# Keeping GpSimd's one-hots and token scatters in traced order, with one scatter in three turns

## The chip, the cores and the metric

The kernel runs on one core of a Trainium2 chip. A core has five engines that each work through their own queue in order: TensorE (PE, matrix products), VectorE (DVE), ScalarE (ACT), GpSimd (POOL) and SyncE (SP, which here only starts transfers). Engines wait for each other by semaphores. The metric is device time in microseconds (us) of one execution, as the median of several runs; less is better. Profiled times are counted from the start of the span of one profiled execution.

## The reference, cut to what matters

Four layers follow each other, each added to x (6250 nodes, 256 features, 100,000 edges). The change is in the seam between the first two.

```python
x = x + gcn(layernorm(x), edges, edge_weight)       # weighted sum over edges, by source; then a two-layer MLP
x = x + moe8(layernorm(x)[None])[0]                 # router, two best of 8 experts
x = x + rgcn(edges, layernorm(x), edge_type)        # sum over edges, by destination
x = x + moe6(layernorm(x)[None])[0]                 # router, two best of 6 experts
```

The sum of the first layer and the router of the second:

```python
msgs = xw[col_sl] * norm[:, None]
h7 = jax.ops.segment_sum(msgs, row_sl, num_segments=N) + b
h = jax.nn.relu(h7 @ W1 + b1)
out = h @ W2 + b2
...
logits = tokens.astype(jnp.float32) @ router_w.astype(jnp.float32).T
probs = jax.nn.softmax(logits, axis=-1)
rw, re = jax.lax.top_k(probs, TOP_K)
```

## The kernel before

Nodes are cut into 49 blocks of 128. An earlier stage has written the message of every edge to device memory (`msgs`), sorted by the block of its source, in 830 tiles of 128 messages. The stage that the change touches, called "sums by source" here, sums them and at the same time starts on the second layer.

`sum_messages` (L944 to L988) takes one tile of messages per **turn**. For a turn, a 128 x 128 one-hot matrix says which row of the block each message belongs to; PE multiplies it with the messages (L983, two passes in the profile), and DVE adds the product to the block's columns of `acc` (L985). Turns go in batches of eight. For each batch one load brings the messages (L950, SP's queue, three batches ahead) and `one_hots` (L953 to L971) makes eight one-hots `m`: DVE computes the keys (L956, marked to keep its order) and makes the first two (L958), ACT the next two (L967 and L968), POOL the last four, one instruction each (L970). The one-hots of the next batch are traced after the second turn of the running one; `m` has two buffers. After every turn the generator yields.

`sum_and_send` (L1270 to L1294) calls `step` once per turn. When a group of four blocks is complete (due at turn 16.46 times the blocks done so far, plus 12, so about every 66 turns), `send_group` starts for it, and each step runs it on to its next `yield`. For four blocks `send_group` works through these steps:

- scale the sums, transpose, MLP, add to X, mean and variance (L1161 to L1191): 11 yields
- normalised tokens `tok` on ACT (L1199), transposes, router products `pl` (L1208): 6 yields
- `route` (L1038 to L1076, with `top`, L1020): a chain of small operations, on DVE but for one exponential on ACT (L1054): 2 yields
- ranks of the tokens at their experts: `both`, `seen` (L1222 to L1231), two small matmuls into `prk` (L1237 and L1240), `place` (L1245 to L1249), and the places in two integer tables `at1` and `at2`, both parts of `ats` (L1255): 2 yields
- the scatters: for each of the four blocks, two indirect transfers issued by POOL (L1259) write its 128 tokens to their two places in `xs`. Before, one yield stands ahead of each pair, so that a group sends two scatters per turn in four turns.

That is 25 yields for a group of four. There are 13 groups: twelve of four blocks and one of one. The last two finish after the last turn. The second layer's experts start when all scatters have landed.

What sets the order: the program is traced in Python, and the framework's scheduler then fixes each engine's queue from the traced order and the dependences, and may put an instruction ahead of or behind others that it doesn't depend on. `tc.keep_in_program_order` marks an instruction that is to keep its traced order among the marked ones of its engine. Before, in this stage, only the keys (L956) are marked. Transfers issued by POOL share its queue with the one-hots. The scatters depend on `tok`, `ats` and nothing else in the stage.

Of the kernel before, what the change touches and what calls it, by code (L numbers as in the profile page):

```python
# [15 lines left out]
OP = mybir.AluOpType  # L16
# [41 lines left out]
def gnn_ffn_kernel(ctx: ExitStack, tc: tile.TileContext, a, out):  # L58
    nc = tc.nc
# [7 lines left out]
    def psum_mm(name):  # L67
        return p_mm.tile([128, 512], F32, tag="mm", name=name)
# [63 lines left out]
    minus = const.tile([128, 128], F32, name="minus")  # L132
# [43 lines left out]
    def blocks_of(blk, t0, engines, top):  # L176
        _, v = nc.values_load_multi_w_load_instructions(
            blk[0:1, t0 : t0 + 8],
            engines=engines,
            min_val=0,  # L180
            max_val=top,
            skip_runtime_bounds_check_because="it is counted or bounded",
        )
        return v
# [176 lines left out]
    with tc.If(unsorted > 0):  # L361
        with tc.tile_pool(name="reorder", bufs=1) as rp:
# [40 lines left out]
            for c in range(EC):  # L403
                ins = nc.gpsimd.indirect_dma_start(
                    out=records,
                    out_offset=bass.IndirectOffsetOnAxis(ap=pos_i[:, c : c + 1], axis=0),
                    in_=rec[:, c, :],
                    in_offset=None,
                )
# [534 lines left out]
    def sum_messages(pool, tag):  # L944

        def take(t0):
            g = pool.tile([128, 8, RW], F32, name=f"g0{tag}_{t0}", tag="g", bufs=4)
            nc.sync.dma_start(g, by_tile[:, t0 : t0 + 8, :])  # L950
            return g

        def one_hots(t0, g):  # L953
            n = min(8, T - t0)
            key = pool.tile([128, 8], F32, name=f"key{tag}{t0}", tag="key")
            tc.keep_in_program_order(nc.vector.tensor_sub(key[:, :n], firsts[:, t0 : t0 + n], g[:, :n, D]))  # L956
            m = pool.tile([128, 8, 128], F32, name=f"m0{tag}_{t0}", tag="m", bufs=2)
            nc.vector.tensor_tensor(  # L958
                m[:, :2],
                minus[:, None, :].to_broadcast([128, 2, 128]),  # L960
                key[:, :2, None].to_broadcast([128, 2, 128]),
                OP.is_equal,
            )
            for j in range(2, n):
                if j < 4:
                    far = pool.tile([128, 128], F32, name=f"far{tag}{t0}_{j}", tag="far", bufs=2)
                    nc.scalar.activation(far, lanes, AF.Abs, bias=key[:, j : j + 1])  # L967
                    nc.scalar.activation(m[:, j], far, AF.Relu, bias=ones[:, 0:1], scale=-1.0)  # L968
                else:
                    nc.gpsimd.tensor_scalar(m[:, j], minus, key[:, j : j + 1], None, op0=OP.is_equal)  # L970
            return m  # L971

        come = {t0: take(t0) for t0 in (0, 8, 16)}
        ready = one_hots(0, come[0])
        for t0 in range(0, TL, 8):
            n = min(8, T - t0)
            blocks = blocks_of(blks, t0, [ENG.DVE], NT)
            if t0 + 24 < TL:
                come[t0 + 24] = take(t0 + 24)
            g, m = come.pop(t0), ready  # L980
            for j in range(n):
                ps = psum_mm(f"pa0{tag}_{t0 + j}")
                nc.tensor.matmul(ps[:, :D], m[:, j, :], g[:, j, :D], start=True, stop=True)  # L983
                here = acc[:, bass.ds(blocks[j] * D, D)]
                nc.vector.tensor_add(here, here, ps[:, :D])  # L985
                if j == 1 and t0 + 8 < TL:
                    ready = one_hots(t0 + 8, come[t0 + 8])
                yield t0 + j + 1  # L988
# [163 lines left out]
    def send_group(g, n, mlp, tag, seen):  # L1152
# [97 lines left out]
        for k, (at, oh) in enumerate(((at1, oh1), (at2, oh2))):  # L1250
            p1 = mlp.tile([128, n], F32, name=f"p{tag}{g}_{k}", tag="p1", bufs=2)
            nc.vector.tensor_reduce(p1, oh, axis=AX.X, op=OP.add)
            if g + n == NT:
                nc.vector.tensor_add(p1[:, n - 1 :], p1[:, n - 1 :], nobody)
            nc.vector.tensor_copy(at[:, g : g + n], p1)  # L1255
        for i, t in enumerate(tiles):
            yield
            for at in (at1, at2):
                ins = nc.gpsimd.indirect_dma_start(  # L1259
                    out=xs,  # L1260
                    out_offset=bass.IndirectOffsetOnAxis(ap=at[:, t : t + 1], axis=0),
                    in_=tok[:, i, :],
                    in_offset=None,
                    bounds_check=8 * CAP - 1,
                    oob_is_err=False,
                )
                tc.declare_no_dep(ins.ins, group=f"tokens{tag}", reason="every token has a place of its own")
                tc.add_to_no_dep_group(f"tokens{tag}", ins.ins)

    def sum_and_send(tag, early):  # L1270


        with (
            tc.tile_pool(name=f"sum{tag}", bufs=3, side="right") as sump,
            tc.tile_pool(name=f"mlp{tag}", bufs=1) as mlp,
        ):
            seen, steps, waiting = [], None, list(GROUPS)

            def step(through):
                nonlocal steps  # L1280
                if steps is None and waiting and through(sum(waiting[0])):
                    g, n = waiting.pop(0)
                    steps = send_group(g, n, mlp, tag, seen)
                if steps is not None and next(steps, steps) is steps:
                    steps = None

            for turn in sum_messages(sump, tag):
                if turn % 8 == 0 and 5 <= turn // 8 < 13:
                    e = turn // 8 - 5
                    nc.sync.dma_start(fw1[:, e], a["L0_ffn_w1"][e].rearrange("(k p) f -> p k f", p=128))  # L1290
                if early:
                    step(lambda blocks: S_TURNS * blocks + S_SLACK <= turn)
            while steps is not None or waiting:
                step(lambda blocks: True)  # L1294
# [66 lines left out]
    for e in range(8):  # L1361
        eng = nc.scalar if e % 2 else nc.sync
        ins = eng.dma_start(xs[bass.ds(ends[e], 128), :], zeros)
# [382 lines left out]
```

## Time and profile before

| | us |
|---|---|
| median of 15 runs | 4037.45 (4034.43 to 4045.95) |
| profiled execution, its time | 4038.73 |
| profiled execution, its span | 4036.9 |

By stretches of that span (busy us of each engine in it):

| stretch, us | what runs | PE | DVE | ACT | POOL | PE clock |
|---|---|---|---|---|---|---|
| 0 to 330 | sorting by source, x times W | 262 | 241 | 146 | 41 | 0.91 |
| 330 to 1280 | most of the messages | 742 | 152 | 348 | 728 | 0.93 |
| 1335 to 2005 | sums by source, with the dispatch | 551 | 494 | 207 | 339 | 0.93 |
| 2030 to 2330 | experts of the second layer | 264 | 111 | 116 | 40 | 0.95 |
| 2700 to 4037 | sums by destination, last experts | 1241 | 759 | 292 | 849 | 0.95 |

How to read it: the busy time is the time in which an engine had an instruction running; the PE clock is the share of its full clock that was granted. Lines of the profile name the engine, the source line, the operation, the tile it writes and the tiles it reads; in brackets stands the idle time ahead of it and what ended that. In the timeline, instructions of one line that follow each other without a pause are merged ("x4").

### The profile page before, as it was taken

What the parts mean: (1) busy time and instruction counts of PE and PEld (TensorE: products, weight loads), DVE (VectorE), ACT (ScalarE), POOL (GpSimd) and SP (SyncE); (2) the same over time, 40 slices, a digit from 0 to 9 for tenths busy, and PEclk for the clock granted to TensorE, in tenths of its full rate; (3) what the DMA queues carried; (4) which work ended last, traced back from release to release, by engine and by line L of the source; (5) the groups of instructions that cost most, each with busy time, mean ns of one, the idle gap of its engine ahead of it and who ended that gap; (6) DMA issues with size and microseconds to landing.
All of it is one profiled execution on the core that took longest, in us unless ns stands there. A gap on an engine that the chain in (4) does not pass through costs nothing.

```text
span 4036.9 us, 53283 instructions
## 1 busy us (share of the span) xinstructions
PE 3430.6 (85%) x14649; PEld 2290.6 (57%) x14649; DVE 2036.7 (50%) x5609; ACT 1322.3 (33%) x3006; POOL 2256.0 (56%) x2450
## 2 busy tenths in 40 slices
PE   7968877777787678888789779996789999999999
PEld 5756656565566355555567534442456666666656
DVE  6872111111111567777723387664556666666552
ACT  3714333333333133233234335662112222221213
POOL 1007777777777455555420185335767777777740
PEclk9989999989999899999899889997889999999999
DMA  3435333333333555555443354446555555555530
GB/s 119 169 106 169 128 126 128 127 128 129 127 129 125 214 180 194 189 193 191 160 127 109 98 188 196 188 203 218 150 140 152 154 147 157 150 151 150 148 108 9
DMA packets 227434, 602.88 MB, mean 149 GB/s; under 512 B 40620, under 2 KB 121689, under 8 KB 207276
## 3 DMA queue, kind: packets, MB, share of 16 engines
q0 software_dynamic: 100736, 295.11, 23.5%
q1 hardware_dynamic: 108242, 287.41, 20.7%
q10 hardware_dynamic: 18138, 16.68, 1.2%
q8 instruction: 132, 2.16, 0.2%
q14 instruction: 186, 1.52, 0.1%
HBM read 362.97 MB, written 236.11 MB: 148 GB/s over the span
## 4 chain that ended last, share of the span: by engine, by line
PE 47%; DVE 14%; DMA 11%; issue 7%; POOL 4%; ACT 3%; DVEq 1%; POOLq 0%; ACTq 0%; SPq 0%
DMA msgs<-msgn,at 8%; PE ph_e1a L246 6%; PE pa1a L1012 6%; PE py1a L1091 6%; PE ph_e2a L246 5%; PE pxn L908 5%; PE phx L1509 4%; PE pa0e L983 4%; DVE acc L985 4%; PE pf L1428 2%; PE pf L1444 2%; POOL msgs L926 2%; DVE rest L1519 1%; DVE sTn L891 1%; DVE acc L1016 1%
## 5 line engine op out<-in xcount | busy, mean ns | idle before, releaser
L1004 POOL DMA_INDIRECT g1a<-hx,idxT x830 | 826.2, 995 | 321.7 <-PE pa1a L1012 145.7
L908 PE MATMUL pxn<-acc,sTn 128*128 x3128 | 788.8, 412 | 245.6 <-DVE sTn L891 237.3
L926 POOL DMA_INDIRECT msgs<-msgn,at x782 | 785.6, 1005 | 270.7 <-DMA msgs<-msgn,at 125.2
L908 PEld LDWEIGHTS pxn<-acc,sTn 128*128 128x128 f32 x3128 | 610.6, 205 | 423.1 <-DVE sTn L891 273.3
L983 PE MATMUL pa0e<-g0e,m0e 128*128 128x256 f32 x1660 | 481.1, 424 | 135.4 <-POOL m0e L970 64.6
L923 ACT ACTIVATE msgn<-pxn,ewT 128x256 f32<-128x256 f32 x782 | 370.8, 474 | 645.2 <-PE pxn L908 451.6
L1016 DVE TENSOR_TENSOR acc<-acc,pa1a 128x256 f32 x830 | 347.0, 418 | 343.5 <-PE pa1a L1012 312.8
L983 PEld LDWEIGHTS pa0e<-g0e,m0e 128*128 128x128 f32 x1660 | 283.9, 200 | 298.3 <-issue 117.4
L899 DVE COPY msgn<-srcT 128x32 f32<-128x32 f32 x98 | 17.7, 184 | 827.9 <-DMA msgs<-msgn,at 747.0
L1012 PE MATMUL pa1a<-g1a,m1a 128*128 128x256 bf16 x2490 | 376.2, 283 | 53.0 <-DMA g1a<-hx,idxT 38.4
L985 DVE TENSOR_TENSOR acc<-acc,pa0e 128x256 f32 x830 | 347.4, 419 | 142.7 <-PE pa0e L983 101.1
L970 POOL TENSOR_SCALAR m0e<-minus,keye 128x128 f32<-128x128 f32 x414 | 251.4, 623 | 278.3 <-PE pa0e L983 125.6
L1012 PEld LDWEIGHTS <-m1a 128*128 128x128 bf16 x2490 | 243.3, 100 | 277.6 <-issue 192.5
L1509 PE MATMUL phx<-wr,xT 128*128 128x512 f32 x784 | 371.0, 617 | 27.4 <-DVE rest L1519 20.9
L1091 PE MATMUL py1a<-w_L_ffn_expert_w,v2a 128*128 128x256 f32 x1176 | 285.7, 383 | 5.9 <-DVE acc L1016 2.9
L246 PE MATMUL ph_e1a<-xT3a,w_L_ffn_expert_w 128*128 128x512 f32 (+2 forms) x672 | 288.1, 555 | 0.0
L253 ACT ACTIVATE v1a<-ph_e1a,cols 128x512 f32<-128x512 f32 (+2 forms) x168 | 106.5, 634 | 537.7 <-PE ph_e1a L246 537.6
L246 PE MATMUL ph_e2a<-v1a,w_L_ffn_expert_w 128*128 128x512 f32 (+2 forms) x672 | 280.5, 543 | 2.1 <-DVE acc L1016 1.3
L1509 PEld LDWEIGHTS phx<-wr,xT 128*128 128x128 f32 x784 | 149.2, 198 | 187.9 <-issue 161.5
L1469 POOL DMA_INDIRECT y<-ys,ats x98 | 96.8, 988 | 277.7 <-issue 262.5
L1091 PEld LDWEIGHTS py1a<-w_L_ffn_expert_w,v2a 128*128 128x128 f32 x1176 | 208.5, 190 | 43.8 <-ACT v2a L253 10.1
L1092 DVE SCALAR_TENSOR_TENSOR X<-py1a,C1a,X 128x256 f32<-128x256 f32 x294 | 138.9, 481 | 112.6 <-PE py1a L1091 111.6
(649 smaller groups left out, 4320.6 us busy)
## 6 DMA issues: line engine op xcount, KB each, us to landing
g0e<-msgs SPq DMA_DIRECT2D x104, 1040.0 KB
hx<-hx SPq DMA_DIRECT2D x49, 1536.0 KB
rowsn<-lane_rows SPq DMA_DIRECT2D x98, 256.0 KB
fx<-xs SPq DMA_DIRECT2D x105, 128.0 KB
ys<-fy ACTq DMA_DIRECT2D x105, 128.0 KB
g1a<-hx,idxT POOLq DMA_INDIRECT x830
msgs<-msgn,at POOLq DMA_INDIRECT x782
msgs<-none SPq DMA_DIRECT2D x10, 650.0 KB
```

The lines of the kernel that those rows point to most:

```text
L246: nc.tensor.matmul(ps[:, :ncols], w[:, k, f * 128 : (f + 1) * 128], xT[:, k, :ncols], start=(k == 0), stop=(k == 1),)
L908: nc.tensor.matmul(come, sT[:, k, j, :], acc[:, bass.ds(blocks[j] * D + k * D, D)], start=(k == 0), stop=(k == 1),)
L923: nc.scalar.activation(msg[:, j, :D], come, AF.Copy, scale=ewT[:, t0 + j : t0 + j + 1])
L926: ins = nc.gpsimd.indirect_dma_start(out=msgs, out_offset=bass.IndirectOffsetOnAxis(ap=at[:, t0 + j : t0 + j + 1], axis=0), in_=msg[:, j, ...
L970: nc.gpsimd.tensor_scalar(m[:, j], minus, key[:, j : j + 1], None, op0=OP.is_equal)
L983: nc.tensor.matmul(ps[:, :D], m[:, j, :], g[:, j, :D], start=True, stop=True)
L985: nc.vector.tensor_add(here, here, ps[:, :D])
L1004: nc.gpsimd.indirect_dma_start(out=g, out_offset=None, in_=table, in_offset=bass.IndirectOffsetOnAxis(ap=idxT[:, t0 + j : t0 + j + 1], axi ...
L1012: nc.tensor.matmul(ps[:, :D], m[:, j, :], g[:, k * D : (k + 1) * D], start=(k == 0), stop=(k == 2))
L1016: nc.vector.tensor_add(here, here, ps[:, :D])
L1091: nc.tensor.matmul(ps[:, :D], hT[:, k, j : j + 128], w[:, k, :], start=(k == 0), stop=(k == 1))
L1509: nc.tensor.matmul(ps, xT[:, k, :], wr[:, k, r : r + 2, :].rearrange("p r o -> p (r o)"), start=(k == 0), stop=(k == 1),)
```

## The change

POOL's one-hots and its scatters are both marked to keep the order in which they are traced. The scatters of a group are no longer traced two per turn: three yields stand ahead of each single one, so that a group of four needs 24 turns for its eight scatters in place of four, and 45 yields in place of 25. What is computed, and by which instructions, stays the same.

```diff
@@ one_hots
-                    nc.gpsimd.tensor_scalar(m[:, j], minus, key[:, j : j + 1], None, op0=OP.is_equal)
+                    tc.keep_in_program_order(
+                        nc.gpsimd.tensor_scalar(m[:, j], minus, key[:, j : j + 1], None, op0=OP.is_equal)
+                    )
@@ send_group
             nc.vector.tensor_copy(at[:, g : g + n], p1)
+
         for i, t in enumerate(tiles):
-            yield
             for at in (at1, at2):
+                yield
+                yield
+                yield
                 ins = nc.gpsimd.indirect_dma_start(
                     out=xs,
                     out_offset=bass.IndirectOffsetOnAxis(ap=at[:, t : t + 1], axis=0),
...
                 tc.add_to_no_dep_group(f"tokens{tag}", ins.ins)
+                tc.keep_in_program_order(ins)
```

## The prediction

> **What bounds the stage now.** I read the page first: PE is busy 85% of the span, so only PE's idle time can be won or lost. The change touches lines that run in one stage, from 1335 to 2005 us. I asked for the groups of that stage, then for the waits, and then for single batches on the timeline. A "batch" is eight turns here: batch k holds turns 8k to 8k+7, GpSimd (POOL) makes the one-hots of its last four turns, so turn 8k+4 is the first that needs POOL.
>
> ```profile
> L983 PE MATMUL pa0e<-g0e,m0e 128*128 128x256 f32 x1660 | 481.1, 424 | 135.4 <-POOL m0e L970 64.6 <-ACT fare L967 34.0 <-DVE acc L985 8.6
> L1259 POOL DMA_INDIRECT xs<-toke,ats x89 | 88.1, 990 | 54.9 <-issue 17.8 <-ACT toke L1199 16.1 <-DVE keye L956 7.9
> ```
>
> ```profile
> PE pa0e L983 <- POOL m0e L970: 64.6, 31, 6.9
> PE pa0e L983 <- DVE seene L1231: 5.6, 7, 1.0
> ```
>
> The stage's PE is idle 135.4 us before its sum matmuls, 64.6 of them for POOL's one-hots (34.0 is the one wait at the stage's start). The timeline of POOL and of PE around the second dispatched group shows where:
>
> ```profile
> 1485.43 2.56 POOL L970 TENSOR_SCALAR m0e<-minus,keye 128x128 f32<-128x128 f32 x4 [2.83 <-DVE r0e L1072]
> 1491.19 1.05 POOL L1259 DMA_INDIRECT xs<-toke,ats  x1 [3.20 <-DVE keye L956]
> 1492.54 0.97 POOL L1259 DMA_INDIRECT xs<-toke,ats  x1 [0.31 <-DVE seene L1227]
> 1493.82 0.97 POOL L1259 DMA_INDIRECT xs<-toke,ats  x1 [0.30 <-issue]
> ...
> 1500.22 0.97 POOL L1259 DMA_INDIRECT xs<-toke,ats  x1 [0.30 <-issue]
> 1501.22 4.67 POOL L970 TENSOR_SCALAR m0e<-minus,keye 128x128 f32<-128x128 f32 x8
> ```
>
> ```profile
> 1490.45 4.52 PE L983 MATMUL pa0e<-g0e,m0e 128*128 128x256 f32 x16 [0.28 <-DVE pe L1252]
> 1501.90 7.62 PE L983 MATMUL pa0e<-g0e,m0e 128*128 128x256 f32 x20 [6.94 <-POOL m0e L970]
> ```
>
> Eight scatters in one run hold POOL from 1491.19 to 1501.19, one each 1.28 us (1492.54 to 1493.82); the one-hots of batch 25 stand behind them, and PE waits 6.94 us. The stage has eleven such waits on the same timeline: 5.13, 6.94, 4.71, 4.71, 5.42, 6.91, 4.33, 4.70, 4.95, 6.44, 4.50, together 58.7 us. In ordinary batches the same place has a gap of 0.25 us.
>
> **What the change moves.** It adds no work: 414 one-hots and 98 scatters before and after. I compared the two kernels' instruction orders, engine by engine. SP's queue (its loads of messages too) and ACT's are the same row for row. POOL's runs of eight are cut up: in ten of the eleven groups into 1, 2 or 3 scatters ahead of the one-hots of some batch k, then two more pieces ahead of those of k+1 and k+2; the second group has 1, 3, 4 around batches 22, 23, 24. The price is in where they went: in those ten the first piece now stands three or four batches earlier than the old run (in the second group ahead of batch 22's one-hots instead of batch 25's). A scatter needs its places, `ats` (L1255), which come at the end of a chain of small DVE operations from L1052 on with two rank matmuls (L1237, L1240) in it. Before, that chain was threaded between the sum adds of about twenty turns; its matmuls stood behind turns 190 and 192, `ats` behind the add of turn 193. Now PE's queue has both rank matmuls right behind turn 179, and DVE's has 27 rows of the chain between the adds of turns 179 and 180. So PE cannot start turn 180 before the rest of the chain is done, then one scatter, then one one-hot. The same pattern stands at turns 251, 315, 379, 443, 507, 579, 643, 707 and 771, with 22 to 28 rows left. That is a new wait with nothing beside it: PE has no other matmul queued, DVE no add.
>
> **The new first wait, step by step.** The end of the stage shows the chain running alone, for the last group of one tile:
>
> ```profile
> 2007.20 0.17 DVE L1025 TENSOR_TENSOR key0e_48a<-P0e,pm10e 128x8 f32<-128x8 f32 x1
> 2008.20 0.16 DVE L1024 TENSOR_REDUCE pm20e<-P0e 128x1 f32<-128x8 f32 x1
> ...
> 2009.42 0.22 DVE L1224 TENSOR_SCALAR bothe<-bothe,token 128x8 bf16<-128x8 bf16 x1
> 2009.68 0.16 DVE L1231 TENSOR_TENSOR seene<-seene,bothe 128x8 bf16<-128x8 bf16 x1
> 2009.96 0.17 DVE L1245 TENSOR_TENSOR placee<-prke,region 128x8 f32<-128x8 f32 x1
> ...
> 2010.76 0.24 DVE L1255 CAST ats<-pe 128x1 int32<-128x1 f32 x2
> ```
>
> From L1025 (2007.20) to the end of `ats` (2011.00) it takes 3.8 us. Take off 0.5 for operations that only the last group has (L1224 0.26, L1254 0.2), add 0.6 for three more `seen` adds at a pitch of 0.2, and 0.4 for wider operands (0.19 for 0.17 us, over some 20 rows): 4.3 us. The other groups start later or earlier in the chain: 4.3, 3.2, 3.2, 3.9, 4.3, 4.5, 3.2, 3.45, 4.1, 4.5; mean 3.9. Around it: turn 180 started at 1479.51 before, while the add of turn 179 ended at 1481.40, so the chain's rest begins 1.9 us after PE would have gone on (1.8 to 1.9 in all ten). From `ats` to the scatter 0.21 (1490.98 to 1491.19), the first one-hot 0.6, PE's start 0.05: 0.9. Ten groups: 10 x (1.9 + 3.9 + 0.9) = 67, and 17 scatters stand in the ten first pieces, 17 x 1.28 = 22. Together 89 us.
>
> **Later waits in those groups.** POOL does not pause after the first wait: four one-hots take 2.34, then the next piece. With one scatter in the first piece, seven remain before the one-hots of k+2; these are ready 2.34 x 2 + 7 x 1.28 = 13.6 us after PE went on. PE arrives there after 8 turns, seven at 0.85 us (the pitch after a long wait, below) and one at 0.6, and 8 at 0.63: 11.5. Five groups wait 2.1. With two in the first piece it is 0.8 (three groups), with three none (two groups). Sum 13 us. Nothing else queues on POOL in this stage.
>
> **The first group** keeps a run: its pieces are 2 (ahead of batch 14) and 6. Its `ats` came at 1428.79, the scatter at 1429.56; two scatters put batch 14's first one-hot at 1432.7, and PE came there at 1430.7: 2.0. From 1432.1, 2.34 + 6 x 1.28 + 0.6 puts batch 15's first at 1442.7; PE, 8 turns of 0.63 on from 1432.7, comes at 1437.8 and waits 5. Sum 7.
>
> **Taken away.** 58.7 less eleven ordinary gaps of 0.25: 56. And the turns that waited for the chain's pieces (the 5.6 us row above, 0.4 for the rank matmuls): 6.
>
> The sum: 89 + 13 + 7 - 56 - 6 = **+47 us**. Against the profiled execution (span 4036.9, run 4038.73, 1.3 above the median) that is 4085.7; against the median 4037.45 it is 4084.5. I take **4085**.
>
> **The clock after a wait.** After the 6.94 us gap the stretch from 1501.90 to 1508.30 has a granted clock of 0.52, and its turns start 0.85 us apart; the stretch 1490.50 to 1495.00 has 1.00. All eleven old waits are followed by 6 to 14 such slow matmuls, and each group has one long wait before and after, so I count no difference. Bounds from these rows: 3 to 7 turns at 0.85 instead of 0.63, that is 0.7 to 1.5 us more or less for each group, 8 to 16 in all.
>
> The Trainium skill, "TensorE: Matmul & The Clock Gate", section "HAM oscillation — how this bites in real kernels", speaks against this change: no idle gap above some 3.4 us, or the array starts cold again. By that rule the new waits of 8 to 10 us pay the same ramp as the old ones of 4.3 to 6.9, and the waits of 2.1 pay none; its ramp of one window, 3.4 us at half speed, would be an estimate of 1.7 us a wait. The rows here show 2.9 to 6.3 us of slow matmuls, and they decide.
>
> **Unknown costs, both ends.** The chain with PE idle: at least 3.0 us (2008.20 to 2011.00 is 2.8, for the shortest), at most the 9.7 it took threaded between adds (1481.32 to 1490.98), which would add 58 in all; I take the row that ran alone, which it is nearest to. The later waits: 0 to 25 (twice the sum above). The lag of 1.9: 1.5 to 2.4. The likeliest case's own range is then 4068 to 4102.
>
> **Rivals.**
> 1. *It does what its words say* (faster). The chain is done before turn 8k+4 comes, the pieces fit into POOL's idle time (2.47 us in an ordinary batch), and all eleven waits go with their slow turns: -56 - 13 = 3968. For it: POOL is busy 339 of 670 us, and three scatters a batch, 3.8, plus 2.34 nearly fit into 5.04. Against: `ats` would have to come 5.8 us earlier (1.9 + 3.9), and DVE's and PE's orders put it where it is. It decides from the point where `ats` ends before turn 8k+3 does. 0.07.
> 2. *The wait is only moved* (no change). The new first wait is 5.1 like the old. It needs a chain of some 1 us, or an add of turn 8k+3 that doesn't lag; the rows show neither. 4037. 0.04.
> 3. *Worse.* The half clock lasts a batch longer after the longer idle (2 us a group) and every later piece makes PE wait (13 more): 4085 + 33 = 4118. For it: the longest old waits (6.9) have up to 14 slow matmuls. Against: 6.44 has 11, 5.42 has 13, no clear growth. 0.12.
>
> **How the numbers follow.** The likeliest case has 0.77. 0.2% is 8 us, about what a measurement of this kernel tells from no change (its 15 runs lie within 11.5). Faster 0.07, same 0.04, slower 0.89. Range: 4058 to 4110, which leaves out rivals 1 and 2 and most of 3.
>
> **What would show it.** In the changed profile: ten PE gaps of 7.5 to 10.5 us ahead of turn 8k+4, released by POOL's one-hots or by DVE's chain at the rank matmuls, instead of eleven of 4.3 to 6.9; the chain's DVE rows back to back with no add among them; one, two or three scatters between `ats` and those one-hots; five waits near 2 us a batch or two later; the stage 670 us long before, near 717 after, and all other stages unchanged. I am wrong if `ats` ends well before PE reaches turn 8k+4, or if the gaps after it are under 5 us.

## The result, and the profile after

The changed kernel takes 4086.9 us (median of 6 runs, 4083.7 to 4094.5) against 4037.1 us (median of 31) for the kernel before on the same chip. The ratio is 1.0124, with a 95% interval from 1.0114 to 1.0134. That is slower by 49.7 us; the prediction was 4085, in a range from 4058 to 4110.

The profiled execution has a span of 4079.7 us. Its groups of instructions in the changed stage, with the lines that answer to L983 and L1259 of before (busy time, mean ns of one, then the idle time ahead of them and what ended it):

```profile
L985 PE MATMUL pa0e<-g0e,m0e 128*128 128x256 f32 x1660 | 477.7, 428 | 134.1 <-POOL m0e L971 81.7 <-ACT fare L967 30.2 <-DVE acc L987 7.6
L1264 POOL DMA_INDIRECT xs<-toke,ats x91 | 90.8, 998 | 187.9 <-issue 169.0 <-ACT toke L1201 15.2 <-DVE acc L987 2.1
```

The sum matmuls are as many and as long as before, and the idle time straight ahead of them has hardly changed (134.1 for 135.4). That number misleads, because the new waits are split. The waits of the stage show the other half (us in total, times, longest):

```profile
PE pa0e L985 <- POOL m0e L971: 81.7, 39, 6.0
PE prke L1239 <- DVE bothe L1224: 42.4, 11, 4.4
PE prke L1242 <- DVE seene L1233: 4.7, 11, 0.4
```

PE now stands 42.4 us ahead of the first rank matmul, in eleven waits, and again for POOL behind the second. The kernel before had two such waits:

```profile
PE prke L1237 <- DVE bothe L1222: 3.8, 2, 3.4
```

The timeline of PE around turn 180, the second group's place (in brackets the idle time ahead of a row and what ended it):

```profile
1478.28 1.97 PE L985 MATMUL pa0e<-g0e,m0e 128*128 128x256 f32 x8
1484.35 0.18 PE L1239 MATMUL prke<-bothe,beforeh 128*128 128x32 bf16 x1 [4.10 <-DVE bothe L1224]
1484.96 0.18 PE L1242 MATMUL prke<-seene,onesh 128*128 128x32 bf16 x1 [0.42 <-DVE seene L1233]
1488.57 5.85 PE L985 MATMUL pa0e<-g0e,m0e 128*128 128x256 f32 x16 [3.43 <-POOL m0e L971]
1494.72 4.16 PE L985 MATMUL pa0e<-g0e,m0e 128*128 128x256 f32 x16 [0.30 <-POOL m0e L971]
1502.17 9.35 PE L985 MATMUL pa0e<-g0e,m0e 128*128 128x256 f32 x32 [3.29 <-POOL m0e L971]
```

Turn 179 ends at 1480.25 and turn 180 starts at 1488.57: 8.32 us in three pieces, then 3.29 more two batches later. In the same time DVE works through the chain with no add between its rows:

```profile
1481.85 0.18 DVE L1027 TENSOR_TENSOR key0e_4a<-P0e,pm10e 128x32 f32<-128x32 f32 x1
...
1484.36 0.74 DVE L1233 TENSOR_TENSOR seene<-seene,bothe 128x8 bf16<-128x8 bf16 x4
...
1485.85 0.27 DVE L1257 CAST ats<-pe 128x4 int32<-128x4 f32 x2
1489.83 0.42 DVE L987 TENSOR_TENSOR acc<-acc,pa0e 128x256 f32 x1 [3.71 <-PE pa0e L985]
```

And POOL waits for the places with the one-hots of batch 22 behind the scatter in its queue:

```profile
1470.14 2.34 POOL L971 TENSOR_SCALAR m0e<-minus,keye 128x128 f32<-128x128 f32 x4 [2.63 <-PE pa0e L985]
1486.80 1.05 POOL L1264 DMA_INDIRECT xs<-toke,ats  x1 [14.31 <-issue]
1487.89 2.36 POOL L971 TENSOR_SCALAR m0e<-minus,keye 128x128 f32<-128x128 f32 x4
1490.42 1.04 POOL L1264 DMA_INDIRECT xs<-toke,ats  x1 [0.17 <-DVE acc L987]
...
1501.48 4.67 POOL L971 TENSOR_SCALAR m0e<-minus,keye 128x128 f32<-128x128 f32 x8
```

POOL sits idle for 14.31 us, put down to "issue", since nothing the profile names as a releaser ended it; the `ats` that ended 0.68 us earlier is what it needed. Chain, scatter, one-hot, PE: 1481.85 to 1488.57.

I measure the stage from the first sum matmul to the first of the last ten scatters, which stand behind the loop: 659.9 us before (1344.28 to 2004.15), 708.6 after (1342.94 to 2051.55). The 48.7 between them is the whole loss of 49.7 within what a run varies.

### The profile page after: what moved, and what is told of

Its sections match the earlier page's. It is cut to its first block, busy times and chain, and to the rows that moved or that the text cites. A ratio compares the mean times of both kernels' runs of the same rounds, so it can differ in the third digit from the quotient of the medians.

```text
span 4079.7 us, 53282 instructions
## 1 busy us (share of the span) xinstructions
PE 3437.3 (84%) x14649; PEld 2311.3 (57%) x14649; DVE 2046.5 (50%) x5609; ACT 1321.7 (32%) x3006; POOL 2255.4 (55%) x2450
## 4 chain that ended last, share of the span: by engine, by line
PE 45%; DVE 13%; DMA 11%; issue 10%; POOL 4%; ACT 3%; DVEq 1%; POOLq 0%; ACTq 0%; SPq 0%
DMA msgs<-msgn,at 9%; PE ph_e1a L246 6%; PE pa1a L1014 6%; PE py1a L1093 6%; PE ph_e2a L246 5%; PE pxn L908 5%; PE pa0e L985 4%; PE phx L1515 3%; DVE acc L987 3%; PE pf L1434 2%; PE pf L1450 2%; DVE rest L1525 2%; POOL msgs L926 2%; DVE hx L1509 1%; PE pt_fh L234 1%
## 5 line engine op out<-in xcount | busy, mean ns | idle before, releaser
L985 PE MATMUL pa0e<-g0e,m0e 128*128 128x256 f32 x1660 | 477.7, 428 | 134.1 <-POOL m0e L971 81.7
L985 PEld LDWEIGHTS pa0e<-g0e,m0e 128*128 128x128 f32 x1660 | 301.9, 205 | 283.7 <-POOL m0e L971 122.2
L1093 PEld LDWEIGHTS py1a<-w_L_ffn_expert_w,v2a 128*128 128x128 f32 x1176 | 208.2, 190 | 44.0 <-ACT v2a L253 10.3
L967 ACT ACTIVATE fare<-lanes,keye 128x128 f32<-128x128 f32 x208 | 72.9, 394 | 450.1 <-DVE keye L956 438.6
```

Of the source, the lines that this page charges most:

```text
L1093: nc.tensor.matmul(ps[:, :D], hT[:, k, j : j + 128], w[:, k, :], start=(k == 0), stop=(k == 1))
```

## The experiments

No kernel leaves out any work; only the order and the spacing differ. "Waits" in this table is the sum of the gaps above 1 us between PE's sum matmuls ahead of turns 8k+4, from the profiled execution. Other matmuls that run in such a gap are not taken off: in the near and late kernels 6.4 to 7.7 us of the sum is one gap ahead of turn 828, in which PE works 5.0 to 6.3 us for the last groups; and every kernel has the same 2.3 us at turn 84.

| kernel | us, and before beside it | ratio (95%) | stage | waits |
|---|---|---|---|---|
| before | 4037.1 | | 659.9 | 62.2 |
| changed | 4086.9, 4037.1 | 1.0124 (1.0114 to 1.0134) | 708.6 | 127.3 |
| scatters marked, not one-hots | 4035.7, 4036.3 | 1.0000 (0.9990 to 1.0009) | 661.7 | 62.1 |
| one-hots marked, not scatters | 4082.8, 4034.3 | 1.0118 (1.0102 to 1.0135) | 712.9 | 125.1 |
| both marks, old spacing | 4137.1, 4036.3 | 1.0250 (1.0233 to 1.0267) | 762.3 | 172.7 |
| changed, 8 turns later | 4059.3, 4036.3 | 1.0058 (1.0041 to 1.0074) | 682.9 | 98.5 |
| changed, 16 turns later | 4026.0, 4036.3 | 0.9976 (0.9966 to 0.9986) | 650.6 | 58.6 |
| near, two in eight turns | 4359.9, 4353.1 | 1.0013 (0.9996 to 1.0031) | 660.4 | 72.5 |
| near, three in eight turns | 4385.5, 4366.3 | 1.0045 (1.0025 to 1.0065) | 676.6 | 95.0 |
| late, two in eight turns | 4302.9, 4353.1 | 0.9901 (0.9869 to 0.9932) | 604.2 | 12.9 |
| late, three in eight turns | 4299.0, 4353.1 | 0.9879 (0.9852 to 0.9905) | 604.6 | 13.1 |
| the same again | 4317.8, 4366.3 | 0.9874 (0.9853 to 0.9896) | 604.1 | 14.2 |
| the same, a third time | 3980.1, 4034.3 | 0.9863 (0.9846 to 0.9879) | 604.5 | 13.8 |

On two of the chips the whole program, before too, was 8% slower; the stage was not (604.6 and 604.1 there, 604.5 on the chip with 4034). So stages can be compared over chips, and times only within a row.

### Which mark does it

The first kernel leaves the scatters' mark and takes off the one-hots':

```diff
-                    tc.keep_in_program_order(
-                        nc.gpsimd.tensor_scalar(m[:, j], minus, key[:, j : j + 1], None, op0=OP.is_equal)
-                    )
+                    nc.gpsimd.tensor_scalar(m[:, j], minus, key[:, j : j + 1], None, op0=OP.is_equal)
```

> The changed kernel with the mark on the one-hots taken off; the mark on the scatters and the three yields per scatter stay. Theory A (on record: PE waits because one-hots stand in POOL's queue behind scatters whose places are not yet computed): in the built program POOL's queue is the one of before, runs of eight scatters ahead of batches 15, 25, 34, 42 and so on, and the rank matmuls stand where they stood, so 4037, within 8. Rival B (the cost lies in tracing a group over 24 turns, which every later piece of the group pays): about 4085. Rival C (a mark on a scatter costs by itself): between the two, above 4045.

4035.7 against 4036.3: nothing changed, as theory A had it. Its counterpart takes off the scatters' mark and leaves the other:

```diff
-                tc.keep_in_program_order(ins)
```

> The changed kernel with the mark on the scatters taken off; the mark on the one-hots and the three yields stay. In the built program every engine's queue is that of the changed kernel. If the one-hots' mark alone brings the cost: 1.0124 of before, as the changed kernel (1.010 to 1.015; 4087 where before takes 4037). If the scatters' mark has a part in it: less than 1.010.

1.0118, the changed kernel's loss. The one-hots' mark alone brings all of it. Tracing a group over 24 turns costs nothing as long as the scheduler may put its scatters behind the one-hots again.

### More scatters behind the same wait

Both marks, with the old spacing:

```diff
         for i, t in enumerate(tiles):
+            yield
             for at in (at1, at2):
-                yield
-                yield
-                yield
                 ins = nc.gpsimd.indirect_dma_start(
```

> Both marks, but the old spacing: one yield for two scatters, 25 yields a group. In the built program the scatters come in runs of 8, 8, 4+4, 8, 8, 8, 6+2, 2+6, 8, 8, 6+2 and the routing chain again has 22 to 31 rows left ahead of turn 8k+4. Theory A: ten waits of 1.9 + 3.9 + 0.9 plus 66 scatters at 1.28 = 151, some 10 for the first group's run of eight and 4 for second pieces, less the 62 that the kernel before waits: +103, so 4140 (4120 to 4160). A wait behind eight scatters should be 16 to 18 us long. Rival B (what costs is that POOL goes to and fro between one-hots and scatters at some thirty places in place of ten): with about as few places as before, 4037 to 4050.

4137.1, 3 from theory A's sum and 90 from rival B's. The timelines of PE and of POOL at turn 180 of this kernel:

```profile
1487.99 0.19 PE L1242 MATMUL prke<-seene,onesh 128*128 128x32 bf16 x1 [0.43 <-DVE seene L1233]
1500.53 4.69 PE L985 MATMUL pa0e<-g0e,m0e 128*128 128x256 f32 x11 [12.35 <-POOL m0e L971]
```

```profile
1489.83 1.05 POOL L1262 DMA_INDIRECT xs<-toke,ats  x1 [14.31 <-issue]
...
1498.84 0.97 POOL L1262 DMA_INDIRECT xs<-toke,ats  x1 [0.30 <-issue]
1499.84 4.67 POOL L971 TENSOR_SCALAR m0e<-minus,keye 128x128 f32<-128x128 f32 x8
```

POOL's 14.31 us and the chain are those of the changed kernel; then eight scatters stand ahead of the one-hots and not one. The whole gap is 17.25 us instead of 8.32: seven scatters at 1.28. The ten first waits come to 153.9 (151 expected). The spread that the change brought along thus softens the loss; the mark with the old spacing costs twice as much.

### Less of the chain left

The changed kernel, with eight more yields ahead of a group's first scatter:

```diff
+        for _ in range(8):
+            yield
         for i, t in enumerate(tiles):
```

> The changed kernel with eight more yields ahead of a group's first scatter. The pieces on POOL stay as they are (first pieces 1, 3, 2, 2, 1, 1, 3, 2, 1, 1), one batch later for the groups after the first; the first group's run of eight is back ahead of batch 15. The routing chain has gone on for eight more turns by then: 2 to 17 rows of it are left ahead of turn 8k+4, 73 in ten groups against some 250 in the changed kernel. Theory A: ten first waits of 1.9 + 0.9, plus 73 rows at 0.155, plus 17 scatters at 1.28 = 61 in place of 90; later waits about 20; less 54 and 3 of before: +24, so 4061 (4045 to 4075). Rival B (the spread scatters themselves, whatever they wait for): as the changed kernel, 4085.

4059.3 for 4061. The sum holds, but two of its terms were off, in opposite senses: the first waits are 72.9 and not 61, and PE wins some of it back afterwards, as below. Most of the 12 us is the lag: from PE's last sum matmul to the end of its add it is 2.2 to 3.3 us in this kernel, 27.7 in ten groups where 19 were counted, since DVE is behind with its adds when the end of the chain stands among them. The rows left behind that add took 11.9, for the 11 counted.

### The places nearly in time

With sixteen yields instead of eight, the chain stands where it stood before:

> The changed kernel with sixteen more yields ahead of a group's first scatter, both marks and one scatter in three turns. In the built program the rank matmuls and the end of the routing chain stand where they stood before, and the scatters go to POOL in pieces of one to four behind them. Theory A: no first wait is left. POOL is idle for 6.8 - 4 x 0.6 = 4.4 us of a batch, so pieces of up to three scatters (3.8) are hidden and a piece of four (5.1) costs about 1 us at each of some five places; ten waits of before are gone (54, less ten spaces of 0.25): 4037 - 51 + 5 = 3991 (3978 to 4005), faster than both. Rival B (scatters spread among the one-hots cost by themselves): 4085. Rival D (a spread scatter is hidden, but PE then waits for the next thing, the messages or DVE's sums, at the same places): 4030 to 4040.

4026.0: faster than both kernels, but by 10 us and not 45. No theory named that. Rival D's number is near, but not its cause, since PE still waits for POOL. DVE, POOL and PE ahead of turn 524 (batch 65) of this kernel:

```profile
1744.82 0.25 DVE L1257 CAST ats<-pe 128x4 int32<-128x4 f32 x2
```

```profile
1745.77 1.03 POOL L1266 DMA_INDIRECT xs<-toke,ats  x1 [9.50 <-ACT m0e L968]
1746.84 2.36 POOL L971 TENSOR_SCALAR m0e<-minus,keye 128x128 f32<-128x128 f32 x4
```

```profile
1742.79 0.68 PE L985 MATMUL pa0e<-g0e,m0e 128*128 128x256 f32 x2
1747.53 8.72 PE L985 MATMUL pa0e<-g0e,m0e 128*128 128x256 f32 x28 [4.06 <-POOL m0e L971]
```

`ats` no longer comes late by a chain, but it comes in the very batch whose one-hots stand behind the scatter: `ats` ends at 1745.07, and PE has been out of one-hots since 1743.47. Ten such waits of 1.5 to 4.1 us come to 30, waits above 1 us for later pieces add 21, and the first group, whose run of eight this kernel still has, 5.1. Two causes were open: the places are still late, or three scatters do not fit into a batch.

### Near or late, two or three

The next kernels separate the two. The scatters are handed to the turns that follow, a few in eight turns, each queued behind the last one-hot traced, at the earliest 26 ("late") or 10 ("near") turns after the chain was traced:

```diff
@@ one_hots
+                    hot[:] = [nc.gpsimd.tensor_scalar(m[:, j], minus, key[:, j : j + 1], None, op0=OP.is_equal)]
+                    tc.keep_in_program_order(hot[0])
@@ send_group
+        def scatter(at, t, i):
+            with tc.issue_after(hot[0].ins):
                 ins = nc.gpsimd.indirect_dma_start(
...
+        sends.extend((clock[0] + 26, at, t, i, scatter) for i, t in enumerate(tiles) for at in (at1, at2))
@@ sum_and_send
+                    if turn % 8 in (3, 5, 7) and sends and sends[0][0] <= turn:
+                        send()
```

`send` takes the first of `sends` and issues it. The kernels with two scatters in eight turns have `(3, 6)` in place of `(3, 5, 7)`, the near ones `+ 10` in place of `+ 26`.

The expectations stand in the order late with three, near with two, late with two, near with three; the last was made when the others were known.

> One-hots marked as in the changed kernel, but a group's scatters are handed over to the turns that follow: the first at the earliest 26 turns after the routing chain was traced, three in eight turns, and each is queued behind the last one-hot traced, so that POOL has one-hots, two or three scatters, one-hots. The first piece stands ahead of batch 17, 25 or 26, 34, 42 and so on, about a batch later than with sixteen more yields. What is open is why that kernel came to 4026 and not 3991. Theory A2 (two inputs were wrong: the places were still not computed when the first scatter stood at POOL's head, ten waits of 1.5 to 4.1, together 30; and an undisturbed batch of PE is 5.0 long, not 6.8, so POOL is idle for 2.6 of it and a third scatter is not hidden): the first waits vanish, a piece of three (3.8) leaves up to 1.2 at some 22 places, less where a batch carries pieces of a group's work: 3980 + 10 to 26, so 4000 (3988 to 4010). Theory D (the time given free is taken by something else, messages, DVE or a lower granted clock): 4020 to 4036.

> As the kernel with three scatters in eight turns, but two in eight turns, and the first at the earliest 10 turns after the chain was traced: first pieces of one or two ahead of batches 15, 24, 32, 40, 48, 57 and so on, where the places are computed in the same batch. Theory A2: ten or eleven first waits stay, 3 to 6 each with two scatters, together 35 to 50 (in four groups the end of the chain is pulled ahead of turn 8k+4); pieces of two (2.5) are hidden behind 2.6: 3980 + 35 to 50, so 4020 (4010 to 4032). If only the number of scatters in a piece mattered and not when the places are computed: 3985.

> Two scatters in eight turns, the first at the earliest 26 turns after the chain was traced: pieces of two ahead of batches 17 to 21, 26 to 29, 34 to 37 and so on, one to two batches after the places are computed. Theory A2: no scatter waits for its place and no piece is longer than the 2.6 that POOL is idle in a batch, so all eleven waits of before (58.7) are gone and nothing takes their place: 4036 - 58.7 + 11 x 0.25 = 3980 (3972 to 3990), faster than both kernels by 1.4%. Theory D: 4020 to 4036, with PE waiting for messages, DVE or at a lower granted clock in the same batches.

> Three scatters in eight turns, the first at the earliest 10 turns after the chain was traced: the fourth of the set near or late, two or three. In the built program the first pieces are 1 to 3 scatters ahead of batches 23, 32, 40, 48, 56, 65, 73, 81, 89 and 98, and the end of the chain is pulled ahead of turn 8k+4 in eight groups. Late, pieces of three cost nothing more than pieces of two (stage of 599.6 against 599.2). Theory A3 (a piece of three behind a first wait costs again, because PE runs through its stock of one-hots at 4.0 to 4.9 a batch after the wait): ten first waits of 6.6 to 8.7, together 72, and later waits of 17: stage of 599 + 72 + 17 - 6 = 682, so 34 over before (25 to 45). Theory A4 (later waits come with the pieces themselves): as late, nothing: stage of 667, 19 over before (10 to 24).

(The expectations of these kernels count the stage from the first to the last sum matmul: 648.1 before, 599.2 and 599.6 late.) Late, both are 1.0 to 1.2% faster than before, and two scatters or three make no difference (604.2 and 604.6 in the table). So the second half of theory A2, that a third scatter is not hidden, falls. Its first half holds: near, with two in a piece, ten waits of 4.6 to 7.1 come back (59.5 together, above the 35 to 50 expected) and the whole gain is gone: 1.0013 of before, where the range expected ends at 4032, just below before. Near with three is 19.2 slower than before, where A3 had 34 and A4 19. The loop of that kernel took 671.6 from its first to its last sum matmul, 682 by A3 and 667 by A4; yet its later waits are there, 15.8 us of them, as A3 said. A4's number is nearer because PE gets most of such a wait back; its claim, that second and third pieces cause no wait, does not hold. They do behind a first wait, and, as the late kernels show, only there.

The late kernel was run twice more:

> The kernel with three scatters in eight turns, the first at the earliest 26 turns after the chain was traced, once more, in five rounds: 48 of before's 648 in the stage are gone. On a chip on which before takes 4037: 3988 (3980 to 3996); on one where it takes 4353: 4303 (4293 to 4308).

> The kernel with three scatters in eight turns, the first at the earliest 26 turns after the chain was traced, beside the kernel with the one-hots marked alone. 54 below before by the stage: 0.987 of before (0.985 to 0.989), so 3983 where before takes 4037.

0.9874 and 0.9863. The third has 3980.1 against 4034.3 and is the version that beats both kernels. Its groups and its waits in the stage:

```profile
L986 PE MATMUL pa0e<-g0e,m0e 128*128 128x256 f32 x1660 | 466.8, 411 | 82.5 <-ACT fare L969 31.6 <-DVE acc L988 16.1 <-POOL m0e L972 5.9
```

```profile
PE pa0e L986 <- POOL m0e L972: 5.9, 20, 0.4
PE pa0e L986 <- DVE seene L1236: 5.3, 6, 1.0
```

PE's waits for POOL are 5.9 us instead of 64.6 and 81.7, none above 0.4. POOL and PE around its second group:

```profile
1483.56 1.05 POOL L1264 DMA_INDIRECT xs<-toke,ats  x1 [3.20 <-PE pa0e L986]
1484.65 2.35 POOL L972 TENSOR_SCALAR m0e<-minus,keye 128x128 f32<-128x128 f32 x4
1487.17 1.04 POOL L1264 DMA_INDIRECT xs<-toke,ats  x1 [0.17 <-issue]
1488.51 0.97 POOL L1264 DMA_INDIRECT xs<-toke,ats  x1 [0.30 <-DVE keye L958]
1489.79 0.97 POOL L1264 DMA_INDIRECT xs<-toke,ats  x1 [0.30 <-issue]
1490.79 2.35 POOL L972 TENSOR_SCALAR m0e<-minus,keye 128x128 f32<-128x128 f32 x4
```

```profile
1482.82 4.52 PE L986 MATMUL pa0e<-g0e,m0e 128*128 128x256 f32 x16 [0.28 <-DVE pe L1257]
1487.94 4.49 PE L986 MATMUL pa0e<-g0e,m0e 128*128 128x256 f32 x16 [0.60 <-DVE acc L988]
```

Three scatters and four one-hots fill POOL from 1487.17 to 1493.14, longer than a batch of PE's, and still PE goes from batch to batch with gaps of 0.3 to 0.6: a second piece eats a lead of POOL's that a first wait would have used up.

## Why the prediction was right

**The mechanism.** The scatter stands ahead of one-hots it has no part in, its places come at the end of a chain, and PE waits for the chain, the scatter and a one-hot. More scatters behind the same wait (17.25 for 8.32), less of the chain left (+23 for +50) and places in time (no wait at all) each moved the time by about the sum made for it. Four sums missed. The 3991 for the kernel with sixteen more yields missed by taking "the chain is where it was" for "the places are there in time". The 4000 for late with three counted a third scatter that PE does not see (0.9879 of before, or 3987, measured). Of the near kernels, the sum for two in eight turns had the first waits too small (35 to 50 for 59.5), and the sum for three (34, measured 19.2) left out what PE gets back after a wait.

**New first waits.** Ten gaps were predicted, 89 us: they are 8.32, 10.12, 8.82, 9.39, 8.31, 8.65, 10.30, 9.05, 8.40 and 8.65, together 90.0. The chain with PE idle in the second group, predicted 4.3, took 4.27 (1481.85 to 1486.12). From `ats` to the scatter it is 0.68 and not 0.21; the lag came out at 1.6 (1480.25 to 1481.85) and not 1.9, so the two errors nearly cancel. Over the ten groups the terms hold one by one: the lag comes to 19.3 us (19 counted), the rest of the chain to 37.4 (39), and the time from the end of `ats` to PE's start to 33.3 (31). **First group:** 2.16 and 4.53, together 6.7, for the 7 predicted.

**Later waits.** Here a term was mis-sized. Predicted were 13 us: five of 2.1, three of 0.8, two none. Measured are 27.8, in all ten groups, the longest 4.11. The time at which POOL has the one-hots of batch k+2 was right: 13.6 us after PE went on, and PE did go on 13.60 after (1488.57 to 1502.17). What failed is PE's pace in between. Turns 180 to 187 took 5.85 us and not 6.55, as five of them were slow and not seven; and the step "8 at 0.63" is wrong: turns 188 to 195 run their sixteen matmuls in 4.16 us, 0.52 a turn. The likely reason is that DVE has no rows of the chain left to put between its adds (nine instructions in that stretch, in the row from 1494.72 below; in the kernel before, twelve from 1490.50 to 1495.00); no run tests this by itself. PE arrives earlier, so it waits longer, and that costs nothing, since POOL sets when it goes on. Against the late kernel's stage the changed one's is 104.1 longer; take off 90.0 and 6.7 and add the 6 below, and some 13 are left for the later waits, the slow turns and the faster turns together. That this is the number predicted is partly luck, since the prediction had only the first of the three in it, at half its size.

**Taken away.** 56 for the eleven old waits: the late kernel, which has none, has a stage 55.4 shorter than before. The other 6, for turns that wait for the chain's pieces, stay in the late kernel (5.3 in its row for `seene`), so it cannot test them. In the changed kernel these pieces come while PE waits anyway, so the 6 belong with that sum.

**The clock.** No difference was counted, and the slow stretch after a wait did not grow with the wait. The windows of the stretch after turn 180's wait in the changed kernel (8.32) and in the kernel with both marks and the old spacing (17.25); columns are the stretch, its length, busy time of PE, PEld, DVE, ACT and POOL, the granted clock, the DMA share and GB/s:

```profile
1488.57:1492.00 3.43, 3.43 (x8) 2.81 (x9) 1.26 (x3) 0.00 (x0) 2.96 (x5) 0.50 0.05 19
1494.72:1498.90 4.18, 4.16 (x16) 2.71 (x16) 3.16 (x9) 1.10 (x4) 3.70 (x5) 1.00 0.79 276
```

```profile
1500.53:1503.96 3.43, 3.43 (x8) 2.81 (x9) 1.26 (x3) 0.00 (x0) 3.43 (x7) 0.50 0.06 20
1504.10:1508.00 3.90, 3.89 (x17) 2.97 (x15) 2.91 (x8) 1.28 (x4) 1.92 (x4) 0.92 0.70 226
```

Eight matmuls take 3.43 us at half clock in both, and the half clock ends 4.3 and 4.2 us after PE goes on. Three to six turns (6 to 13 matmuls) are slow after each of the ten first waits of either kernel; after the old waits it was 6 to 14 matmuls. That is against rival 3, "the half clock lasts a batch longer".

What the count of "no difference" missed is the number of such stretches. In the kernel before, the clock falls to half around eleven waits; in the changed kernel around eighteen: the ten first waits, the two of the first group and six of the later ones. Of the 1660 sum matmuls 185 start at half clock in place of 131. The stretch after the wait of 3.29 us ahead of turn 196, in which the clock is at half from 1503.15 to 1506.56:

```profile
1502.17:1506.00 3.83, 3.83 (x10) 2.78 (x11) 1.69 (x4) 0.00 (x0) 3.83 (x7) 0.63 0.16 60
```

What these turns cost by themselves is not shown; it lies within the 13 us that are left above. The Trainium skill, "TensorE: Matmul & The Clock Gate", section "HAM oscillation — how this bites in real kernels", says that the array starts cold again after an idle gap of more than about 3.4 us. The ten first waits, of 8.3 us and more, agree with it. But waits of 2.00 us (turn 332), 2.16 (turn 116), 3.28 (turns 460 and 724) and 3.29 (turn 196) were followed by 3.4 us of half clock too, and waits of 2.01 (turn 660) and 2.47 (turn 396) were not; so the length of a gap alone does not decide here, and "the waits of 2.1 pay none" does not hold.

**The rivals.** Rival 1 (the change does what its words say) named its own condition: `ats` done before turn 8k+3 ends. The changed kernel does not meet it; the late kernel does, and is 54 us below before where the rival had 69. The 13 us for the slow turns were too much: the late stage is shorter by the old waits alone. Rival 2 needed gaps of 5.1; the ten are 8.3 to 10.3. Of rival 3, second pieces do make PE wait again, but at no net cost beyond the sum.

**What would show it.** Ten gaps of 7.5 to 10.5, the chain's rows back to back, one to three scatters ahead of the one-hots, a stage some 47 longer: seen. "Five waits near 2 us" was wrong. "All other stages unchanged" holds within some 6 us: the profiled spans differ by 42.8, the stage by 48.7, the medians by 49.7.

**What the words of the change hide.** The description of the mark given above, that it keeps the order among marked instructions, is too strong. The two marked kernels show it: marked scatters alone stay where the scheduler puts them, and marked one-hots alone carry the whole effect. In the framework's source the mark ties an instruction to the one traced just before it on its engine. For a one-hot that can be a scatter, which then has to go first. For a scatter it is, in the built program, a small instruction that reads a register for it, which is free to move. That would be why the pieces come as 1, 3, 4 and not in even threes, and why a scatter can be pulled forward but not held back; no run tests it by itself. Queueing each scatter behind the last one-hot holds it from the other side.

One thing stays open: how much of the late kernel's gain needs the even pieces. A kernel with the plain yields, traced late enough, was not run.

## What to carry to other kernels

Ahead of pinning two kinds of work in one engine's queue, ask what each of them waits for. Instructions with late inputs (here transfers whose addresses end a long chain) must be traced behind the point where these are ready, counted in turns of the engine that must not stop; pieces that fit, and a chain in its old place, are not enough. Then compare the order of all engines, since the scheduler pulls the chain forward to serve the pinned instruction: the loss shows on PE and DVE, two engines away from the edit. When a row's idle time is unchanged and the stage is longer, look for the wait ahead of another line.

## What was not expected of the hardware

- After gaps of 8.3 and of 17.3 us the half clock ended alike, 4.3 and 4.2 us after PE went on; from 8 us on, a longer idle time brought no longer slow stretch. Waits as short as 2.0 us (turn 332 of the changed kernel) were followed by one of 3.4 us.
- With no waits for POOL the granted clock of the whole stage rises. The window of the changed kernel and that of the late kernel in its third run (columns as above):

```profile
1335.00:2050.00 715.00, 554.31 (x2266) 385.04 (x2266) 502.42 (x1854) 206.43 (x623) 338.16 (x502) 0.90 0.50 179
```

```profile
1335.00:1960.00 625.00, 547.88 (x2287) 349.03 (x2287) 506.33 (x1924) 207.53 (x626) 349.91 (x515) 0.97 0.58 209
```

0.97 for 0.90. By the rows of the two kernels' groups above, the 1660 sum matmuls take 466.8 us of PE's time in place of 477.7.

- Chips differ in the stages around, by 8% for the same program, and not in this one (604.6, 604.1, 604.5). From 1000 to 1300 us, in the stage that makes most of the messages, the two chips with the longer times moved 111 to 114 GB/s where another moved 128.
